# Two graph layers on one core: the order of the first and last steps, a factor row made on TensorE, and one final check

## The chip, the cores and the metric

The kernel runs on one core of a Trainium2 chip. The metric is the device time of one execution in microseconds. Before the change it is 3325.57 us, the median of three runs (3324.71 to 3328.04).

## The reference

64 graphs of 256 nodes with 512 features each go through three attention steps. All numbers are float32.

```python
# layer 0, 8 heads of 64
Q, K, V = x @ W_q + b_q, x @ W_k + b_k, x @ W_v + b_v
scores = Q K^T / 8 + a_i + c_j + b_g + log(adj + 1e-9)      # a, c = x @ w_g halves
x = softmax(scores) V + x
# layer 1, attention one (8 heads), then attention two (1 head, W2), each:
h = layer_norm(x) @ W
s, t = sum(h * a_src), sum(h * a_dst)                        # per node and head
e = leaky_relu(s_i + t_j, 0.2) + adj
x = softmax(e) h + x
```

## The kernel before

**Stages of one graph.** `graph(b)` is a Python generator. Each `yield` ends a step, and `order` lists which graph runs its next step. The steps of one graph are, in this order: "load" (x and adjacency), "turn" (transposes on VectorE, the sums S for a Winograd product on GpSimd, a copy of xT stored in DRAM); "V", "V7", "V4", then the same three for Q and for K (seven block products instead of eight; `winograd`, L294 to L344); "scores" twice (four heads each, L562, with the exponentials L569 on ScalarE); "mask" twice (the exponentials times the adjacency, L583, and their sum over the two halves, L588); "sums 0" (`weight_sums`: column sums by a matmul with ones, L371, their reciprocal L378, stored to DRAM and read back spread over the partitions as R, L381 and L386; it also fetches the stored x); "product 0" (weights times V, L404); "gather 0" (products times R plus bias and x, L413 and L418, then S and the store); "tokens 1" (transposes back, L253, for the norm's mean and variance on ScalarE, and its root on GpSimd, L276); "V1", "V1 7", "V1 4"; "rows 1" (`target_rows`, L423); eight "weights" (two instructions L658 each); "sums 1", "product 1", "gather 1", "tokens 2"; "V2", "V2 7", "V2 4", "rows 2", "weights 2" (two instructions L709) and twice "product 2" (L721, L726, L728, and four output stores L737).

**Factor rows.** The leaky exponent is written as a maximum of two products, so that a row of exp(-0.8 s) over all nodes is needed on every partition. `target_rows` makes it for eight heads and for one head alike: an exponential on ScalarE (L426), a 32x32 block transpose on VectorE (L428), four stores to DRAM (L431), and a load that spreads the row over the partitions (L441).

**Weights of layer 1.** `fold_norm` folds the norm into W1 and W2 in three steps for each: "transpose" loads two vectors spread over the partitions (L175), multiplies them with W on GpSimd in four products (L181) and reduces these on VectorE (L185). "columns" makes `left` (L192, L193), multiplies on TensorE (L197), and sends the sums through DRAM (L203 to L220). "totals" scales W (L226), forms its block differences (`combine`, L128) and transposes a small tile (L231). W1's 16 loads are traced as soon as graph 1 exists or "transpose" is reached, W2's likewise with graph 2 (L843 to L848).

**What sets the order.** TensorE runs in the order written: `start`, then a `period` of 40 steps repeated for all graphs, then `finish` (L741 to L817). The instructions of the other engines, SyncE's transfers among them, are ordered by a scheduler that takes them in the order of the program as they become ready in its own model of time; on the chip every queue then runs in the order so fixed. Tiles with one tag share a fixed number of buffers. The tag "ET" (four) holds the products of `fold_norm` and the exponentials of layers 0 and 1. The tag "X2" (four) holds the spread vectors, `left`, the token form of x for the last attention, and `bad` in `note_odd`. All matmul results share one ring of eight PSUM banks.

**Checks.** Extremes of sums and exponents are kept on the way (L348, L389, L390, L733, L734). `note_odd` (L351) compares a tile with a lower and an upper bound, three instructions for each. It is called for four tiles after the last graph's "rows 2" (L858 to L863), and for `last_top` and `last_bottom` at the end (L867). From `odd` follows a count of graphs (L869 to L876) to be done again in a slower form, whose loop runs that many times.

## Time and profile before

| what | us |
|---|---|
| median of three runs | 3325.57 |
| the profiled execution | 3324.74 |
| its span, first to last instruction | 3322.9 |
| TensorE busy, 0 to 200 | 152.08 |
| TensorE busy, 200 to 3200 | 3000.00 |
| TensorE busy, 3200 to 3322.9 | 94.66 |
| VectorE busy, whole span | 2443.8 |

PE is TensorE, PEld its weight load, DVE VectorE, ACT ScalarE, POOL GpSimd, SP SyncE, whose queue issues nearly all transfers. A line of a timeline shows the start, the time until the last of the group ends, the engine and line, the operation, what it writes from what, how many there are, and in brackets how long the engine idled before it and what ended that. A line of the list of waits shows who waited for whom: us in total, how many times, the longest.

### The profile page before, as it was taken

To read this page: it belongs to the slowest core of one execution; us is meant where nothing else is said; L and a number is where in the kernel's file an instruction comes from. 1 tells how busy PE (TensorE), PEld (TensorE's weight loads), DVE (VectorE), ACT (ScalarE), POOL (GpSimd) and SP (SyncE) were. 2 spreads that over 40 slices of the span, in tenths; PEclk is the share of its full clock that TensorE was granted. 3 is DMA by queue.
4 is the path that set the end of the run, shared out by engine and by line. 5 is a ranking of instruction groups with operands and counts; after the bars stand their busy time and mean duration, and the time that the engine had idled before them with its cause. 6 is when DMAs were issued, how large, how long until landed. Compare 5 with 4: busy or idle time off the path is not lost.

```text
span 3322.9 us, 80192 instructions
## 1 busy us (share of the span) xinstructions
PE 3246.7 (98%) x31044; PEld 2746.7 (83%) x31044; DVE 2443.8 (74%) x5273; ACT 1453.7 (44%) x4039; POOL 935.3 (28%) x1247
## 2 busy tenths in 40 slices
PE   5899999999999999999999999999999999999997
PEld 3788888888888888888888888888888888888875
DVE  4667777777777777777777777777777777777775
ACT  2344444444444444444444444444444444444442
POOL 3122322322322322322322322322322323223222
PEclk8999999999999999999999999999999999999998
DMA  5324334334333334334343343343333243343332
GB/s 132 96 76 119 105 90 119 100 95 113 103 99 113 99 102 113 93 108 111 90 114 107 91 115 101 97 114 103 92 117 105 89 119 106 89 119 104 91 97 64
DMA packets 271825, 341.26 MB, mean 103 GB/s; under 512 B 108608, under 2 KB 187728, under 8 KB 271440
## 3 DMA queue, kind: packets, MB, share of 16 engines
q1 hardware_dynamic: 270672, 335.53, 35.4%
q8 instruction: 248, 4.06, 0.5%
q14 instruction: 137, 1.12, 0.1%
q10 hardware_dynamic: 768, 0.54, 0.1%
HBM read 233.61 MB, written 102.31 MB: 101 GB/s over the span
## 4 chain that ended last, share of the span: by engine, by line
PE 94%; DVE 2%; DMA 1%; SPq 1%; issue 1%; ACT 0%; POOL 0%; ACTq 0%; DVEq 0%; POOLq 0%
PE ps_a L310 20%; PE ps_a L317 14%; PE ps_num L404 13%; PE ps_b L310 10%; PE ps_b L317 7%; PE ps_sc L562 7%; PE ps_av L721 6%; PE ps_su L371 5%; PE ps_c L310 5%; PE ps_tr L253 4%; PE ps_c L317 3%; SPq L121 1%; DMA R<-kept 1%; DMA kept<-inverse 0%; DVE ET L583 0%
## 5 line engine op out<-in xcount | busy, mean ns | idle before, releaser
L658 DVE SCALAR_TENSOR_TENSOR ET<-R,f,EA 128x256 f32<-128x256 f32 x1024 | 463.2, 518 | 138.0 <-PE ps_num L404 136.9
L404 PE MATMUL ps_num<-ET,V 128*32 128x256 f32 x8192 | 466.9, 380 | 0.0
L404 PEld LDWEIGHTS ps_num<-ET,V 128*32 128x32 f32 x8192 | 264.3, 110 | 155.1 <-issue 1.3
L583 DVE TENSOR_TENSOR ET<-ET,AT 128x1024 f32<-128x1024 f32 x256 | 304.2, 1222 | 78.8 <-ACT ET L569 78.8
L569 ACT ACTIVATE ET<-ps_sc,V 128x512 f32<-128x512 f32 x512 | 303.1, 702 | 90.2 <-PE ps_sc L562 90.0
L390 POOL TENSOR_TENSOR added<-added,inverse 128x128 f32<-128x128 f32 x128 | 69.3, 541 | 861.9 <-DVE inverse L378 745.2
L310 PE MATMUL ps_a<-w,S 128*128 128x264 f32 (+1 forms) x1024 | 273.3, 389 | 1.1 <-ACT m L607 1.1
L310 PE MATMUL ps_b<-w,S 128*128 128x264 f32 (+1 forms) x1024 | 266.5, 383 | 0.0
L721 PE MATMUL ps_av<-V,ET 128*128 128x258 f32 (+1 forms) x1024 | 247.0, 385 | 5.6 <-DVE ET L709 5.6
L286 POOL TENSOR_TENSOR S<-yT 128x256 f32<-128x256 f32 x64 | 64.0, 1000 | 666.2 <-PE ps_su L371 595.5
L562 PE MATMUL ps_sc<-QT,KT 64*128 64x256 f32 x2048 | 241.2, 385 | 0.0
L310 PEld LDWEIGHTS ps_a<-w,S 128*128 128x128 f32 x1024 | 187.1, 189 | 51.4 <-issue 19.2
L562 PEld LDWEIGHTS ps_sc<-QT,KT 64*128 64x128 f32 x2048 | 193.4, 188 | 42.5 <-issue 21.8
L310 PEld LDWEIGHTS ps_b<-w,S 128*128 128x128 f32 x1024 | 193.9, 189 | 31.0
L721 PEld LDWEIGHTS ps_av<-V,ET 128*128 128x128 f32 x1024 | 187.9, 193 | 29.1 <-DVE ET L709 4.5
L413 DVE TENSOR_TENSOR ps_num<-ps_num,R 128x512 f32<-128x512 f32 x256 | 165.6, 692 | 57.3 <-DMA R<-kept 53.5
L679 POOL TENSOR_TENSOR X<-X,bw 128x512 f32<-128x512 f32 x128 | 160.0, 1270 | 164.4 <-ACT X L268 164.4
L646 DVE TENSOR_TENSOR V<-V,factors 128x256 f32<-128x256 f32 x256 | 196.0, 824 | 0.0
L270 ACT ACTIVATE ps_tr<-ps_tr,less 128x512 f32<-128x512 f32 x256 | 165.7, 647 | 0.1
L486 ACT ACTIVATE EA<-AT 128x512 f32<-128x512 f32 x64 | 40.4, 631 | 279.5 <-DVE ET L709 265.7
L614 ACT ACTIVATE V<-ps_a,rstd 128x257 f32<-128x257 f32 (+1 forms) x128 | 61.2, 478 | 220.2 <-PE ps_a L310 220.2
L588 DVE TENSOR_TENSOR total<-ET 128x1024 f32<-128x1024 f32 x128 | 153.8, 1201 | 0.0
(166 smaller groups left out, 6987.0 us busy)
## 6 DMA issues: line engine op xcount, KB each, us to landing
R<-kept SPq DMA_DIRECT2D x128, 512.0 KB
X<-in_x_dram SPq DMA_DIRECT2D x256, 128.0 KB
kept<-xT SPq DMA_DIRECT2D x64, 512.0 KB
yT<-kept SPq DMA_DIRECT2D x64, 512.0 KB
R<-kept SPq DMA_DIRECT2D x512, 64.0 KB
kept<-yT SPq DMA_DIRECT2D x64, 512.0 KB
out_dram<-X SPq DMA_DIRECT2D x512, 64.0 KB
zT<-kept SPq DMA_DIRECT2D x63, 512.0 KB
```

The lines of the kernel that those rows point to most:

```text
L270: nc.scalar.activation(pt, pt, AF.Square, bias=less[:, of], accum_out=squares[:, of])
L310: nc.tensor.matmul(to, A[:, kk, :], B[:, kk, :], start=(first and kk == 0), stop=(kk == 1), skip_group_check=not first,)
L317: nc.tensor.matmul(to[:, m * P : (m + 1) * P], B[:, kk, m * P : (m + 1) * P], A[:, kk, :], start=(first and m == kk == 0), stop=(kk == 1), ...
L371: nc.tensor.matmul(pt[32 * g : 32 * g + 32, :P], columns[:, at - 8 * i : at - 8 * i + 32], weights[:, i % 2 * P : i % 2 * P + P], start=(i ...
L404: nc.tensor.matmul(num[32 * a : 32 * a + 32, m * N : (m + 1) * N], V[:, j, a // 2, a % 2 * P + q * DH + 32 * m :][:, :32], pair[a // 2][:, ...
L413: nc.vector.tensor_tensor(both, both, R[:, q, :].unsqueeze(1).to_broadcast([P, 2, N]), ALU.mult)
L562: nc.tensor.matmul(banks[h % 2][:, o : o + N], KT[lo : lo + DH, (q + h) // 2, j * P : (j + 1) * P], QT[lo : lo + DH, (q + h) // 2, :], sta ...
L569: nc.scalar.activation(ET[:, j, i::2, :], banks[i].rearrange("p (h n) -> p h n", n=N), AF.Exp, bias=c[:, j, :],)
L583: nc.vector.tensor_tensor(ET[:, j, :, :], ET[:, j, :, :], AT[:, j, :].unsqueeze(1).to_broadcast([P, 4, N]), ALU.mult,)
L646: nc.vector.tensor_tensor(v, v, factors8[:, at : at + H // 2, :1].to_broadcast([P, H // 2, DH]), ALU.mult)
L658: nc.vector.scalar_tensor_tensor(ET[:, j, h, :], R[q][:, h, :], f[:, j, at : at + 1], EA[:, j, :], ALU.max, ALU.mult,)
L721: nc.tensor.matmul(av[:, :width], ET[:, j, t * P : (t + 1) * P], V2[:, j, n, :width], start=(j == 0), stop=(j == NT - 1),)
```

## The change

The lists `start` and `finish` hold the same steps in another order; `period` is as before. For the last graph, "rows 2" makes the factor row without DRAM: the exponential is written to a tile of its own, VectorE copies it 128 times wide, and TensorE multiplies this copy, as the stationary operand, with the identity, which leaves the row on every partition of a PSUM bank; L709 reads it there. The two tiles for the last check become one tile `extremes`, checked by one call.

```diff
-    last_top = const.tile([P, NT], F32, name="last_top")
-    last_bottom = const.tile([P, NT], F32, name="last_bottom")
-    for t in (last_top, last_bottom):
-        nc.gpsimd.memset(t, 1.0)
+    extremes = const.tile([P, 2, NT], F32, name="extremes")
+    nc.gpsimd.memset(extremes, 1.0)
...
         def target_rows(st, heads, b):
+            if heads == 1 and b == B - 1:
+                e = small.tile([P, NT], F32, name="last_rows", tag="last_rows")
+                nc.scalar.activation(e, st[:, :, 0, 0], AF.Exp, scale=-0.8)
+                wide = data.tile([P, NT, P], F32, name="wide", tag="R1")
+                nc.vector.tensor_copy(wide, e.unsqueeze(2).to_broadcast([P, NT, P]))
+                pt = ps("row")
+                for t in range(NT):
+                    nc.tensor.matmul(
+                        pt[:, t * P : (t + 1) * P], wide[:, t, :], ident, start=True, stop=True
+                    )
+                return [pt[:, :N].rearrange("p (h n) -> p h n", h=1)]
...
-                    nc.vector.tensor_tensor(last_top, last_top, rinv, ALU.max)
-                    nc.vector.tensor_tensor(last_bottom, last_bottom, rinv, ALU.min)
+                    for i, op in enumerate((ALU.max, ALU.min)):
+                        nc.vector.tensor_tensor(extremes[:, i], extremes[:, i], rinv, op)
...
         start = [
-            (0, "load"), (0, "turn"), (0, "V"), (0, "V7"), (0, "V4"), (0, "Q"), (0, "Q7"),
-            (0, "Q4"), (0, "K"), (0, "K7"), (0, "K4"), (1, "load"), (1, "turn"),
-            ("w1", "transpose"), ("w2", "transpose"), (0, "scores"), (1, "V"), ("w1", "columns"),
-            (0, "scores"), ("w1", "totals"), (0, "mask"), (0, "mask"), ("w2", "columns"), (1, "V7"),
-            (0, "sums 0"), (0, "product 0"), (1, "V4"), (0, "gather 0"), (2, "load"), (2, "turn"),
-            (1, "Q"), (1, "Q7"), (0, "tokens 1"), (1, "Q4"), (1, "K"), (1, "K7"), (1, "K4"),
-            (0, "V1"), (0, "V1 7"), (0, "V1 4"), (1, "scores"), (0, "rows 1"), ("w2", "totals"),
-            (1, "scores"), (1, "mask"), (0, "weights"), (1, "mask"), (2, "V"), (2, "V7"),
-            (1, "sums 0"), (1, "product 0"), (1, "gather 0"), (0, "weights"), (2, "V4"), (2, "Q"),
+            (0, "load"), (0, "turn"), (0, "V"), (0, "V7"), (0, "V4"), (0, "Q"), (1, "load"),
+            (0, "Q7"), (0, "Q4"), (0, "K"), (0, "K7"), ("w1", "transpose"), (0, "K4"),
+            (0, "scores"), (0, "scores"), (1, "turn"), (0, "mask"), (0, "mask"), (1, "V"),
+            (1, "V7"), ("w1", "columns"), (1, "V4"), (0, "sums 0"), (0, "product 0"),
+            (0, "gather 0"), (1, "Q"), (1, "Q7"), ("w1", "totals"), (1, "Q4"), (0, "tokens 1"),
+            (1, "K"), (1, "K7"), (2, "load"), (1, "K4"), (0, "V1"), (0, "V1 7"), (0, "V1 4"),
+            ("w2", "transpose"), (2, "turn"), (1, "scores"), (0, "rows 1"), (1, "scores"),
+            ("w2", "columns"), (1, "mask"), (0, "weights"), (1, "mask"), (2, "V"), (2, "V7"),
+            ("w2", "totals"), (1, "sums 0"), (1, "product 0"), (1, "gather 0"), (0, "weights"),
+            (2, "V4"), (2, "Q"), (0, "weights"), (0, "weights"), (2, "Q7"), (0, "weights"),
...
         finish = [
...
-            (-2, "weights"), (-1, "mask"), (-2, "weights"), (-4, "V2"), (-4, "V2 7"), (-4, "V2 4"),
-            (-1, "sums 0"), (-1, "product 0"), (-1, "gather 0"), (-4, "rows 2"), (-2, "weights"),
-            (-2, "weights"), (-2, "weights"), (-2, "weights"), (-4, "weights 2"), (-3, "product 1"),
-            (-1, "tokens 1"), (-3, "gather 1"), (-4, "product 2"), (-3, "tokens 2"), (-1, "V1"),
+            (-2, "weights"), (-2, "weights"), (-1, "mask"), (-4, "V2"), (-4, "V2 7"), (-4, "V2 4"),
+            (-1, "sums 0"), (-4, "rows 2"), (-4, "weights 2"), (-3, "product 1"), (-2, "weights"),
+            (-2, "weights"), (-2, "weights"), (-2, "weights"), (-1, "product 0"), (-1, "gather 0"),
+            (-2, "weights"), (-3, "gather 1"), (-4, "product 2"), (-1, "tokens 1"),
+            (-3, "tokens 2"), (-1, "V1"), (-1, "V1 7"), (-4, "product 2"), (-1, "V1 4"), (-3, "V2"),
...
-            (-1, "product 1"), (-3, "product 2"), (-1, "gather 1"), (-1, "tokens 2"), (-2, "V2"),
-            (-2, "V2 7"), (-2, "V2 4"), (-2, "rows 2"), (-1, "V2"), (-2, "weights 2"), (-1, "V2 7"),
-            (-1, "V2 4"), (-1, "rows 2"), (-1, "weights 2"), (-2, "product 2"), (-2, "product 2"),
-            (-1, "product 2"), (-1, "product 2"),
+            (-1, "tokens 2"), (-2, "V2"), (-2, "V2 7"), (-2, "V2 4"), (-2, "rows 2"), (-1, "V2"),
+            (-2, "weights 2"), (-1, "V2 7"), (-2, "product 2"), (-1, "V2 4"), (-1, "rows 2"),
+            (-1, "weights 2"), (-2, "product 2"), (-1, "product 2"), (-1, "product 2"),
...
-        for v in (last_top, last_bottom):
-            note_odd(v, 1e-25, 1e25)
+        note_odd(extremes.rearrange("p i t -> p (i t)"), 1e-25, 1e25)
```

Further on, both lists differ in where single steps "load", "weights", "turn", "gather" and "mask" stand. A negative number counts from the end: -1 is the last graph, -2 the one before.

## The prediction

> **What bounds the kernel.** The page first: one engine fills the span.
>
> ```profile
> span 3322.9 us, 80192 instructions
> PE 3246.7 (98%) x31044; PEld 2746.7 (83%) x31044; DVE 2443.8 (74%) x5273; ACT 1453.7 (44%) x4039; POOL 935.3 (28%) x1247
> ```
>
> The stretches say where the missing 2% lies (columns: stretch, length, busy time of PE, PEld, DVE, ACT, POOL, granted clock, DMA share, GB/s).
>
> ```profile
> 0.00:200.00 200.00, 152.08 (x1258) 121.63 (x1259) 114.13 (x216) 61.06 (x164) 50.28 (x74) 0.91 0.37 102
> 1700.00:3200.00 1500.00, 1500.00 (x14473) 1275.30 (x14471) 1127.86 (x2427) 679.37 (x1887) 427.47 (x567) 1.00 0.36 104
> 3200.00:3322.90 122.90, 94.66 (x831) 73.03 (x829) 74.59 (x210) 36.47 (x111) 30.14 (x40) 0.91 0.24 73
> ```
>
> From 200 to 3200 TensorE never idles, so nothing can be won there. It idles 47.9 us before and 28.2 after (6.9 of these follow its last matmul). The list of waits names them for the first 205 us:
>
> ```profile
> PE ps_fold L197 <- ACT left L192: 13.1, 1, 13.1
> PE ps_su L371 <- DVE total L588: 8.6, 2, 6.3
> PE ps_a L310 <- ACT u L495: 3.9, 1, 3.9
> PE ps_fold L231 <- DMA chunks<-bw: 3.6, 1, 3.6
> PE ps_tr L253 <- DVE yT L418: 2.3, 2, 2.1
> ```
>
> The timelines say why. w1's fold waits for `left` (L192), the third user of a buffer that holds the vector w1's third product on POOL reads:
>
> ```profile
> 56.39 0.30 ACT L192 COPY left<-columns 128x128 f32<-128x128 f32 x1 [13.15 <-POOL product L181]
> 49.41 9.25 POOL L181 TENSOR_TENSOR product<-w,vector 128x1024 f32<-128x1024 f32 x4 [8.46 <-DMA vector<-in_L_gnn_a_src_dram]
> 62.16 1.22 DVE L185 TENSOR_REDUCE w<-product 128x2 f32<-128x1024 f32 x1 [2.24 <-POOL product L181]
> 63.41 4.73 ACT L569 ACTIVATE ET<-ps_sc,V 128x512 f32<-128x512 f32 x8
> 82.52 1.71 PE L371 MATMUL ps_su<-total,ones 128*32 128x128 f32 x26 [6.32 <-DVE total L588]
> ```
>
> Graph 0's exponentials (L569) start at 63.41 though their scores were done at 39: `ET` shares its tag and four buffers with the products of both folds, and the first product of w2 is reduced at 62.16 + 1.22 = 63.38. So w2's fold holds graph 0 back, to 82.5. At the other end:
>
> ```profile
> 3237.11 2.15 PE L253 MATMUL ps_tr<-ident,yT 128*128 128x128 f32 x8 [4.94 <-DVE yT L418]
> 3298.38 5.28 PE L721 MATMUL ps_av<-V,ET 128*128 128x258 f32 x16 [1.51 <-DVE ET L709]
> 3307.75 5.42 PE L721 MATMUL ps_av<-V,ET 128*128 128x258 f32 x16 [4.08 <-DVE ET L709]
> 3315.66 0.37 PE L871 MATMUL ps_tr<-ident,odd 128*1 128x128 f32 x1 [2.50 <-DVE odd L358]
> ```
>
> **The start, step by step.** Up to 37.1 the order is the same. SP is busy issuing without a break to 43.8 in both (wv, wq, wk, graph 1's X and A, then w1's 16 loads): bringing (1, "load") forward gains nothing, since SP already issues it at 27.9, as soon as it can.
>
> New: w1's transpose comes before w2's and before (1, "turn"). Its two vectors leave SP at 43.85 instead of 44.41, ahead of graph 1's 512 KB store and not followed by w2's 16 loads; I take them 2 us earlier at POOL, 47.4 for 49.41 (bounds 0 and 3: the first one now takes 5.0 from issue to use). Four products of 2.3 and reductions of 1.22 then run to 57.9. `left` now finds a free buffer, so the fold's first matmuls start when two reductions are through, the rest at 57.9; 32 matmuls, 3.5 us: done at 61.5 (before: 62.8).
>
> Graph 0's scores are now both ahead of it: 37.1 to 41.0. Their exponentials wait for the first and second product of w1 instead of w2: 47.4 + 2.3 + 1.2 = 50.9 and 53.2, eight of 0.59. PSUM is a ring of 8 banks: (1, "V") takes those of the first scores, so TensorE stands from 41.0 to about 51.5, one wait of 10 for one of 13.1. V and V7 (5.2, slow at first) run into the fold. DVE meanwhile: four reductions to 57.9, four masks and two totals of 1.2 each, two puts of 0.43, some of it between the reductions: 65.5. "sums 0" (1.0) and "product 0" (3.45) end at 70.0. Before: 88.8, of which w2's columns (3.7) come later now. **Gain 88.8 - 3.7 - 70.0 = 15.1.** If the exponentials need not wait, (1, "V") is done sooner, but the reductions still bind: 68, gain 17. If DVE runs two of w2's reductions ahead of the masks, as it does now, some 5 more: gain 10.
>
> Behind it: w2's 16 loads and two vectors, at 0.64 each 11 us of SP, go while SP waits for w1's sums (45 to 61) or just after; its products need two buffers that "product 0" frees at 70, so 75 for the last; its columns are reached at about 95: hidden by 20 us. If SP keeps them behind (2, "load"), whose adjacency waits for graph 1's turn (about 66), they leave SP from 68 to 80 and are reduced by 92: a cover of 3 us. Beyond it each us late is a us lost. w2's "totals" now stand 5.2 us of matmuls (V, V7) behind its columns; w1's row shows 7.05 from the fold's end (62.76) to the chunks (69.81): a wait of 1.9, in place of the 2.28 on "sums 0" at 125.7, since both end there. w2's scaling and differences, 8 x 0.41 + 4 x 0.67 = 6.0 of DVE, lay in DVE's idle time; now they fall where DVE is full (114 to 134): I charge 1.1, bounds 0 and 6, low since only "tokens 1" stands behind. POOL's S factors can queue behind a 2.3 us product: 0 to 2, in that charge. **Start: -14.**
>
> **The end.** Product 2 of graph -4 now comes before "tokens 1" of the last graph. It wants R(-4), issued by SP at 3231.57 behind the four R loads and landed near 3235, and fills 1.7 of the wait of 4.94. But ET(-4) (1.34 of DVE) may go ahead of yT and move it by 1.6. The chain goes on through ACT (rstd), V1, rows 1, 16 weights and T0 = 3289.95, the end of (-2, "V2 4"). Bounds -2 and +0.3: I take **-1.0**. The other moves of the finish ((-1, "load") earlier, weights and masks among each other) leave TensorE's order as it was, and lie before 3224, where it is full: nothing, unless rival (e) holds.
>
> From T0 before: R(-2) lands, product 2 at T0 + 8.4; the last R at 3307.12; last matmul at 3313.2 = T0 + 23.2. Removed for the last graph: transpose, four stores (3299.25 to 3301.57), R (3303.96 to 3307.12), that is 8.1 us and five SP issues. Added: one copy on DVE (256 wide; rows of 0.42 to 0.48, say 0.4) and two matmuls, 4 passes of 0.11 as L317's eight take 0.89: 0.45; with hops 1.1. The copy's buffer is R's, free once graph -2's L709 has run, which stands before. After: product 2 of -2 moves ahead of (-1, "V2 4"), so TensorE waits 3.2 for it, to T0 + 8.4. The Trainium skill ("TensorE: Matmul & The Clock Gate", "What's actually happening") has half rate only after an idle window of about 3.4 us; by that 3.2 could stay fast and the step take 1.74. But the row at 3298.38 took 5.28 for 16, where 3.5 is full rate, after a wait of 1.51. I take the row: step 3.5; the rule would make the sum 1.7 less. V2 4 to T0 + 12.9, then ACT, copy, two matmuls (TensorE stands 1.6 of it) T0 + 15.1, product 2 of -2 to 16.9, of -1 to 20.4: 2.8 before T0 + 23.2.
>
> But DVE has its own bill: the checks called after (-1, "rows 2"), 24 instructions, 4.7 us, whose `bad` (X2 tag, four buffers, all held by the last two graphs) waits for graph -2's first out store, near 3306; then three half products 3.7, the last check. Called before "weights 2", they can even push L709 behind them (up to 4.7). Last check: one note is 6 instructions instead of 12, -0.8 at 0.14. DVE's 9.4 from 3306.2 ends at 3315.6, as before (3315.5), if nothing of it starts sooner; TensorE's side would give -3.6. Between: **-1.5**. The 6.4 from the count to the span's end stay.
>
> **Sum**: 14 + 1.0 + 1.5 = 16.5. The profiled execution took 3324.74; 3308.2. It lies 0.8 under the median 3325.57, so **3309**.
>
> **Rivals.** (a) As above, 3304 to 3313: 0.53. (b) Free exponentials and a tail set by TensorE: 17 + 2 + 5 = 24: 3301; the products' early place in every queue speaks against it. 0.20. (c) The moved fold makes its own waits (DVE's 6.0 in full, w2's reductions ahead of masks) and the checks hold L709: 10 - 2 + 1 = 9: 3317. DVE busy 16.5 of the 20 us from 120 to 140 speaks for it. 0.18. (d) Waits only change names, within 0.2% (6.7 us, about what a measurement of this kernel tells from none): 0.05. (e) Slower: the middle has no slack (1500 of 1500), and the other engines' order there follows from the start's. If it leaves even one wait per graph, of 50.2 us each, it counts some 59 times in these 3000 us: from 0.28 us a graph the gain of 16.5 is gone, at 0.45 the result is 3335. DVE at 75% there speaks against it. 0.04.
>
> Faster is (a), (b) and (c), 0.91; within 0.2% is (d), 0.05; slower is (e), 0.04. The range leaves out (d), (e) and the edges of (b) and (c), about 0.1: 3299 to 3318.
>
> **What would show it.** L569 of graph 0 starting near 51 and "product 0" ending near 70, w2's columns near 95 without a wait; full TensorE again from about 190; no SP row for the last graph's L431 and L441; L709's last pair 2 to 3 us after V2 4. Wrong if L569 still follows a reduction of w2, if TensorE waits on L231 or L253 for over 4 us after 95, if L356 runs ahead of the last L709, or if any wait stands between 200 and 3180.

## The result, and the profile after

The changed kernel takes 3319.49 us (median of 17 runs, 3314.46 to 3322.07) where the kernel before takes 3326.13 (17 runs). The ratio is 0.9981, 95% interval 0.9974 to 0.9988: 6.6 us less, where 16.5 were forecast. The profiled execution took 3316.03 us with a span of 3314.3, so it lies 3.5 below its own median, and what is read from one trace below is held against the others.

In the changed kernel the lines have moved: L310 is L309, L371 is L370, L404 L403, L253 L252, L197 L196, L185 L184, L569 L580, L588 L599, L616 L627, L709 L720, L721 L732, L871 L882, L495 L506, L507 L518. New are L429 (the row's copy), L432 (its matmuls) and L745 (the extremes).

The stretches first (stretch, length, busy time of PE, PEld, DVE, ACT, POOL, granted clock, DMA share, GB/s):

```profile
0.00:200.00 200.00, 156.63 (x1307) 127.93 (x1307) 120.21 (x227) 64.83 (x175) 54.39 (x77) 0.94 0.38 109
1700.00:3180.00 1480.00, 1480.00 (x14293) 1258.92 (x14295) 1112.87 (x2390) 667.91 (x1852) 417.85 (x556) 1.00 0.36 104
3180.00:3314.30 134.30, 106.65 (x977) 82.15 (x969) 82.07 (x227) 42.46 (x128) 34.39 (x46) 0.92 0.24 74
```

The middle is still full, at full clock (200 to 1700 too: 1500.00 of 1500.00), so whatever changed lies in the two ends; the rival in which every graph gains a wait is out. In the first 200 us TensorE is busy for 4.55 us more than before, where 14 us of idle and slow time were to go. The list of TensorE's waits over the whole span names what it waits for now (engine, tile and line, what it waited for, us in total, times, longest; rows of the first loads left out at the dots):

```profile
PE ps_a L309 <- ACT ET L580: 10.8, 1, 10.8
PE ps_av L732 <- DVE ET L720: 8.1, 3, 4.2
PE ps_a L309 <- DVE V L518: 5.6, 2, 5.1
...
PE ps_a L309 <- ACT m L506: 4.9, 1, 4.9
PE ps_a L309 <- DVE V L627: 4.7, 4, 2.5
```

The old first place, 13.1 us for `left` of w1's fold, is gone. The first row is the forecast's wait for PSUM banks ("one wait of 10"). The second row stands at the end of the kernel. The third is a wait for VectorE's puts, its copies of finished products out of PSUM; the forecast's sum holds 4.0 us of it (the fold done at 61.5, the puts at 65.5). The fourth, and the fifth, of which 2.5 us stand in the start, were not in the forecast. TensorE's timeline shows them in place, and what the clock did behind them:

```profile
66.31 2.08 PE L309 MATMUL ps_a<-wv,xT 128*128 128x257 f32 x4 [5.07 <-DVE V L518]
68.31 1.76 PE L370 MATMUL ps_su<-total,ones 128*32 128x128 f32 x32
69.90 3.63 PE L403 MATMUL ps_num<-ET,V 128*32 128x256 f32 x64
...
98.83 1.16 PE L309 MATMUL ps_a<-w,yT 128*128 128x264 f32 x4 [2.48 <-DVE V L627]
...
103.57 1.94 PE L196 MATMUL ps_fold<-w,left 128*32 128x257 f32 x32
...
113.17 2.05 PE L309 MATMUL ps_a<-wv,S 128*128 128x257 f32 x4 [4.87 <-ACT m L506]
115.02 1.92 PE L309 MATMUL ps_b<-wv,S 128*128 128x257 f32 x4
116.73 1.44 PE L309 MATMUL ps_a<-wv,S 128*128 128x257 f32 x4
```

Product 0 of graph 0 ends at 73.5 where it ended at 88.8: 15.3 us sooner, of which w2's columns (3.66 before, 1.94 now, at 103.57) are still owed. Product 0 of graph 1 ends at 122.77 where it ended at 130.25: only 7.5 us sooner. So 13.4 us were won by 73.5, and 5.9 of them were given back in the next 49 us. V4 of graph 1, 1.0 us of TensorE, stood behind product 0 before and stands ahead of it now; with this and w1's totals (0.2) counted where they are done, 14.2 us were won and 6.7 given back.

What stands ahead of the 2.48 us wait is seen on VectorE: w2's reductions (L184), which the change moved here, between the puts of graph 0's V1 (L627):

```profile
96.75 1.22 DVE L184 TENSOR_REDUCE w<-product 128x2 f32<-128x1024 f32 x1 [0.53 <-POOL product L180]
97.89 0.48 DVE L627 SCALAR_TENSOR_TENSOR V<-ps_b,rstd,u 128x264 f32<-128x264 f32 x1
98.29 0.48 DVE L627 SCALAR_TENSOR_TENSOR V<-ps_a,rstd,m 128x264 f32<-128x264 f32 x1
```

At the end of the kernel (same columns):

```profile
3289.26 3.77 PE L732 MATMUL ps_av<-V,ET 128*128 128x258 f32 x8 [3.23 <-DVE ET L720]
...
3296.07 0.71 PE L432 MATMUL ps_row<-ident,wide 128*128 128x128 f32 x4 [1.33 <-DVE wide L429]
3296.62 1.90 PE L732 MATMUL ps_av<-V,ET 128*128 128x258 f32 x8
3299.16 3.73 PE L732 MATMUL ps_av<-V,ET 128*128 128x258 f32 x16 [0.65 <-DVE ET L720]
3306.81 0.37 PE L882 MATMUL ps_tr<-ident,odd 128*1 128x128 f32 x1 [3.91 <-DVE odd L357]
```

The row's transfers are gone and the last product waits 0.65 us in place of 4.08. But the first half of graph -2's product 2, moved ahead of the last graph's V2 4, waits 3.23 us and then runs at half speed, and the transpose of the last check stands 3.91 us for VectorE.

### The profile page after: what moved, and what is told of

It is laid out like the page before. It is cut to its first block, busy times and chain, and to the rows that moved or that the text cites. A ratio compares the mean times of both kernels' runs of the same rounds, so it can differ in the third digit from the quotient of the medians.

```text
span 3314.3 us, 80184 instructions
## 1 busy us (share of the span) xinstructions
PE 3243.3 (98%) x31048; PEld 2746.2 (83%) x31048; DVE 2440.7 (74%) x5267; ACT 1452.7 (44%) x4039; POOL 935.1 (28%) x1246
## 4 chain that ended last, share of the span: by engine, by line
PE 94%; DVE 2%; SPq 1%; DMA 1%; issue 1%; ACT 0%; POOL 0%; ACTq 0%; DVEq 0%; POOLq 0%
PE ps_a L309 20%; PE ps_a L316 13%; PE ps_num L403 13%; PE ps_b L309 10%; PE ps_b L316 7%; PE ps_av L732 7%; PE ps_sc L573 7%; PE ps_su L370 5%; PE ps_c L309 5%; PE ps_tr L252 4%; PE ps_c L316 3%; SPq L120 1%; POOL product L180 0%; DMA R<-kept 0%; SPq L442 0%
## 5 line engine op out<-in xcount | busy, mean ns | idle before, releaser
L669 DVE SCALAR_TENSOR_TENSOR ET<-R,f,EA 128x256 f32<-128x256 f32 x1024 | 461.2, 516 | 136.0 <-PE ps_num L403 134.3
L403 PE MATMUL ps_num<-ET,V 128*32 128x256 f32 x8192 | 466.5, 380 | 0.0
L403 PEld LDWEIGHTS ps_num<-ET,V 128*32 128x32 f32 x8192 | 264.0, 110 | 154.9 <-issue 1.2
L580 ACT ACTIVATE ET<-ps_sc,V 128x512 f32<-128x512 f32 x512 | 303.0, 702 | 102.4 <-PE ps_sc L573 89.5
L309 PE MATMUL ps_a<-w,S 128*128 128x264 f32 (+1 forms) x1024 | 273.4, 389 | 1.1 <-ACT m L618 1.1
L309 PE MATMUL ps_b<-w,S 128*128 128x264 f32 (+1 forms) x1024 | 266.5, 383 | 0.1
L732 PE MATMUL ps_av<-V,ET 128*128 128x258 f32 (+1 forms) x1024 | 246.9, 385 | 8.1 <-DVE ET L720 8.1
L309 PEld LDWEIGHTS ps_a<-w,S 128*128 128x128 f32 x1024 | 186.9, 189 | 51.7 <-issue 19.5
L309 PEld LDWEIGHTS ps_b<-w,S 128*128 128x128 f32 x1024 | 193.8, 189 | 31.5 <-issue 0.4
L732 PEld LDWEIGHTS ps_av<-V,ET 128*128 128x128 f32 x1024 | 187.0, 193 | 31.5 <-issue 8.8
L412 DVE TENSOR_TENSOR ps_num<-ps_num,R 128x512 f32<-128x512 f32 x256 | 165.7, 692 | 52.3 <-DMA R<-kept 49.3
L309 PE MATMUL ps_a<-wv,xT 128*128 128x257 f32 x512 | 142.3, 400 | 21.1 <-ACT ET L580 10.8
L625 ACT ACTIVATE V<-ps_a,rstd 128x257 f32<-128x257 f32 (+1 forms) x128 | 61.2, 478 | 229.0 <-PE ps_a L309 229.0
## 6 DMA issues: line engine op xcount, KB each, us to landing
X<-in_x_dram SPq DMA_DIRECT2D x256, 128.0 KB
```

Source lines behind the costliest of these rows:

```text
L309: nc.tensor.matmul(to, A[:, kk, :], B[:, kk, :], start=(first and kk == 0), stop=(kk == 1), skip_group_check=not first,)
L403: nc.tensor.matmul(num[32 * a : 32 * a + 32, m * N : (m + 1) * N], V[:, j, a // 2, a % 2 * P + q * DH + 32 * m :][:, :32], pair[a // 2][:, ...
L412: nc.vector.tensor_tensor(both, both, R[:, q, :].unsqueeze(1).to_broadcast([P, 2, N]), ALU.mult)
L580: nc.scalar.activation(ET[:, j, i::2, :], banks[i].rearrange("p (h n) -> p h n", n=N), AF.Exp, bias=c[:, j, :],)
L669: nc.vector.scalar_tensor_tensor(ET[:, j, h, :], R[q][:, h, :], f[:, j, at : at + 1], EA[:, j, :], ALU.max, ALU.mult,)
L732: nc.tensor.matmul(av[:, :width], ET[:, j, t * P : (t + 1) * P], V2[:, j, n, :width], start=(j == 0), stop=(j == NT - 1),)
```

## The experiments

The table gives the medians, the ratio to the kernel before, and two marks of each trace: when the first product 2 of graph 0 starts (everything behind it is full until the end, so a change of the start shows here and nowhere later), and the time from the first product 2 of graph -5 to the end of the span (a change of the end shows here alone). From trace to trace of the same steps either mark spreads over some 4 us.

| kernel | median us (runs) | ratio, 95% interval | start mark | end length |
|---|---|---|---|---|
| before | 3326.1 (17) | 1 | 232.8 | 129.0 |
| changed | 3319.5 (17) | 0.9981 (0.9974-0.9988) | 225.4 | 128.1 |
| e1 start only | 3315.9 (7) | 0.9973 (0.9962-0.9985) | 226.4 | 126.5 |
| e2 finish only | 3331.1 (21) | 1.0018 (1.0011-1.0024) | 235.2 | 136.5 |
| e3 copies first | 3319.2 (17) | 0.9980 (0.9973-0.9987) | 226.5 | 131.6 |
| e4 fold back | 3328.3 (21) | 1.0008 (1.0002-1.0015) | 237.3 | 129.5 |
| e5 fold late | 3325.2 (13) | 0.9998 (0.9990-1.0006) | 237.0 | 127.7 |
| e6 old finish, row | 3315.4 (8) | 0.9970 (0.9959-0.9980) | 227.6 | 124.4 |
| e7 e6 + own scratch | 3315.4 (5) | 0.9965 (0.9952-0.9979) | 229.1 | 123.3 |
| e8 no row | 3324.1 (13) | 0.9995 (0.9986-1.0003) | 228.3 | 132.6 |
| e9 one step back | 3316.9 (18) | 0.9977 (0.9970-0.9984) | 227.6 | 130.5 |
| e10 copies, totals | 3319.8 (13) | 0.9988 (0.9980-0.9996) | 225.7 | 128.0 |
| e11 + reductions | 3319.1 (21) | 0.9983 (0.9976-0.9989) | 227.7 | 127.8 |
| e12 e11 + old finish | 3315.0 (9) | 0.9974 (0.9964-0.9984) | 228.8 | 123.2 |
| e13 reductions on ScalarE | 3318.8 (18) | 0.9979 (0.9972-0.9987) | 227.0 | 131.7 |
| e14 + differences on GpSimd | 3319.4 (21) | 0.9982 (0.9976-0.9989) | 228.4 | 128.9 |
| e15 e14 + old finish | 3316.6 (9) | 0.9977 (0.9967-0.9986) | 228.0 | 125.9 |
| e16 two steps back | 3318.4 (21) | 0.9982 (0.9975-0.9988) | 225.8 | 130.6 |
| e17 reciprocal first | 3319.8 (21) | 0.9983 (0.9976-0.9989) | 228.3 | 130.5 |
| e18 e17 + old finish | 3316.1 (7) | 0.9974 (0.9963-0.9985) | 228.8 | 126.4 |

The theory at the outset: the fold of w2, moved out of the first 74 us, makes new waits in the queues of VectorE, ScalarE and SP behind it, and these take back half of the start's gain. The rivals: the loss lies in the first 74 us; or in the end.

**One part alone.**

```diff
  e1: the kernel before
-        start = [ ... ]        # its own first steps
+        start = [ ... ]        # those of the changed kernel
  e2: the kernel before
-        finish = [ ... ]
+        finish = [ ... ]       # those of the changed kernel
```

> The kernel before with the changed kernel's list of first steps alone; the last steps, the factor row and the last checks are as before. Theory 1 (the new start brings 15 us by the end of the first product of graph 0 and gives half of it back behind that, by 123 us): the whole start is worth 7.4 us here too, 3318.7 where before is 3326.1, give or take 1. Theory 2 (the start is worth more, and the new end or the new row takes some of it back): 10 us or more off, 3316 or less. Theory 3 (most of the change's measured 6.6 us are the end's): 4 us off or less, 3322 or more.

> The kernel before with the changed list of last steps alone. Theory 1: the marks of the two traces give the end some 1.2 to 1.5 us (span -8.6, of which -7.4 to -7.8 stand before the last steps start); part of it is the row's and the note's, so 0 to 1.5 us off, 3324.6 to 3326.1. Theory 2 (the new end takes back): 1 to 4 us longer. Theory 3 (the end brings most): 3 to 6 us off.

By its ratio the new start alone takes 9 us off (interval 5 to 13), more than the whole change with its 6.3, though the intervals overlap; the new end alone adds 5.7 (interval 3.7 to 8). For e1 that is nearer to theory 2 than to 1; its start mark says 6.4, and the seven traces with the start as changed have a mean of 227.2 against 234.0 for the two with the old one: 6.8. For e2 theory 2 holds, and by more than it allowed. So the end does not bring 2.5 us; as an order of steps it costs. Why is read from e2's timeline:

```profile
3302.03 3.77 PE L721 MATMUL ps_av<-V,ET 128*128 128x258 f32 x8 [3.10 <-DVE ET L709]
3307.31 2.27 PE L721 MATMUL ps_av<-V,ET 128*128 128x258 f32 x8
3316.56 6.26 PE L721 MATMUL ps_av<-V,ET 128*128 128x258 f32 x16 [6.98 <-DVE ET L709]
```

Product 2 of graph -2 comes first, waits for its weights and runs at half speed, and V2 4 of the last graph, between the first two of these lines, comes some 6 us later than it could: 13.0 us behind V2 4 of graph -2, where it was 6.9. The row of the last graph starts from V2 4, goes through four stores and a load, and the last product now waits 6.98 us for it, where it waited 4.08.

**The end taken apart.** The old order of the last steps with everything else changed; the same with the checks' scratch in two buffers of its own; and the changed kernel without the row on TensorE:

```diff
  e6: the changed kernel
-        finish = [ ... ]
+        finish = [ ... ]       # those of the kernel before
  e7: e6, in note_odd
-    name="bad", tag="X2", bufs=4)
+    name="bad", tag="bad", bufs=2)
  e8: the changed kernel, in target_rows
-            if heads == 1 and b == B - 1:
-                ...
-                return [pt[:, :N].rearrange("p (h n) -> p h n", h=1)]
```

> The changed kernel with the last steps in the order of before: the new start, the row on TensorE and the one note stay. Theory A (the new order of the last steps costs, the row pays): the wait of 4.04 us ahead of the last product in the run with the new start alone falls to about 2 (copy and row matmuls), so 1 to 2 us less than that run, 3314 to 3315, and 4.5 to 5.5 less than the changed kernel. Theory B (the row and the note cost what they save, since VectorE's checks end last anyway): as the run with the new start alone, 3315.5 to 3317. Theory C (the new order pays, once the row is there): the changed kernel's 3319.5 or more.

> The kernel of the run with the new start, the old order of the last steps and the row, where the notes' scratch tile has two buffers of its own in place of the ring that the output tiles use. In the trace of after a check stands 1.4 us behind an output transfer for that ring, and TensorE waits 3.9 us for the last check. Theory A (the checks wait for the ring, and VectorE ends the span): the large checks move into idle time of VectorE, 1.5 to 2.5 us less than without. Theory B (VectorE's time, not the ring, holds them): 0.5 us or less.

> The changed kernel without the row on TensorE: the last graph's factor row goes through VectorE's turn, four stores and a broadcast load as in the kernel before; lists and note stay as changed. If the parts add up (start -9.5, finish +5.7, change as a whole -6.6) the row and the note are worth 2.8 us here, so 3322. If the row is what pays for the new order of the last steps (in the run with that order alone the last product waits 6.98 us for this row, 1.98 in the changed kernel): up to 5 us, 3324.5. If the row is hidden: 3319.5.

e6 is 3.7 us below the changed kernel by the ratios (0.9970 and 0.9981, intervals that overlap a little), and three more pairs, which differ in the order and the scratch, go the same way by their medians: e12 is 4.1 below e11, e15 2.8 below e14, e18 3.7 below e17. That is theory A in its direction; the row's gain over e1 is not shown by the times (0.9970 against 0.9973). e8 is 4.6 above the changed kernel: the row pays where the new order makes the last product wait for it, as its second reading had it. By the medians the four corners of the end are: old order 3315.9, old order and row 3315.4, new order 3324.1, new order and row 3319.5. The row is worth about nothing with the one and 4.6 with the other; the order costs 8 without it and 4 with it.

The traces show the last part of this more evenly than the times. T0 is the end of V2 4 of graph -2; the table has the us from there to the end of the span:

| | old order | new order |
|---|---|---|
| row through DRAM | 32.9 (before), 33.2 (e1) | 38.7 (e2), 37.8 (e8) |
| row on TensorE | 30.5 (e6) | 31.9 to 33.5 (changed, e3, e4, e5, e10, e11, e13, e14, e17) |
| row and own scratch | 28.1 to 28.4 (e7, e12, e15, e18) | not run |

Without the row the new order costs 5 us here. With it, it costs 2.3 against e6, whose product behind the row ran at full clock by luck (3.63 us; 5.32 in e7): at half clock e6 would stand near 32.2, and little would be left of the order's cost behind T0. The row alone is worth 2.6 us in e6, and about 1 at half clock.

e6's timeline shows the order that the forecast did not work out, old steps with the new row:

```profile
3288.35 1.13 PE L309 MATMUL ps_a<-w,xT 128*128 128x257 f32 x4 [0.58 <-DVE V L627]
3291.88 0.68 PE L432 MATMUL ps_row<-ident,wide 128*128 128x128 f32 x4 [2.40 <-DVE wide L429]
3292.40 3.63 PE L732 MATMUL ps_av<-V,ET 128*128 128x258 f32 x16
3296.68 3.73 PE L732 MATMUL ps_av<-V,ET 128*128 128x258 f32 x16 [0.65 <-DVE ET L720]
3305.57 0.37 PE L882 MATMUL ps_tr<-ident,odd 128*1 128x128 f32 x1 [5.16 <-DVE odd L357]
```

V2 4 of graph -2 starts at 3281.43 here, and the last product ends 19.0 us later; in the changed kernel it starts at 3279.69 and the product ends 23.2 later. Graph -2's row lands while the last graph's V2 runs, so nothing needs its product early. In e7 the small checks run in idle time, the wait for the last of them falls to 1.36 us, and from the last matmul to the end it is 8.8 us in place of 12.7, as theory A has it; the medians of e6 and e7 do not differ (3315.4 both), which is theory B. In e7 a check also runs ahead of the row's copy, but the row hardly waits longer for that (2.43 us against 2.40); that product 2 behind it took 5.32 us, not 3.63, is the clock's doing (last section). From T0 the scratch saves 2.2 us in the traces, in spite of that product; that the medians do not show it stays open. The new start, the row and the old last steps (e6, with or without the scratch) are by their medians the versions below both kernels, some 10 us under the one before.

**Which step.** The two products of the finish that moved ahead, put back one after the other:

```diff
  e9: the changed kernel, last steps
-    (-1, "V2 7"), (-2, "product 2"), (-1, "V2 4"), (-1, "rows 2"), (-1, "weights 2"),
+    (-1, "V2 7"), (-1, "V2 4"), (-1, "rows 2"), (-1, "weights 2"), (-2, "product 2"),
  e16: e9, and
-    (-4, "product 2"), (-1, "tokens 1"),
+    (-1, "tokens 1"), (-4, "product 2"),
```

> The changed kernel with one step of its last steps moved back: the first product 2 of graph -2 stands behind the last graph's V2 4, rows 2 and weights 2 again, as in the order before; the row and the note stay. In the trace of after TensorE waits 3.23 us for that product's weights, runs it slowly in 3.6, and reaches V2 4 only then, so that the row comes 15.4 us behind graph -2's V2 4; in the run with the whole old order it comes 9.5 us behind it. Theory (this one step is what the new finish costs): 3 to 4.5 us less than the changed kernel's 3319.5, so 3315 to 3316.5. Rival (the other early product, of graph -4 ahead of the last graph's tokens 1, costs as much: the stretch up to the end of graph -1's first product of weights and V1 is 31.9 us in place of 30.2 to 30.9): 1.5 to 3 less, 3316.5 to 3318.

> The changed kernel with two of its last steps moved back: the first product 2 of graph -2 behind the last graph's weights 2 (as in the run before with that alone), and the first product 2 of graph -4 behind the last graph's tokens 1. If these two are all that the new order of the last steps costs: as with the whole old order, 3315.4, give or take 1, 1 to 2 us below the run with one of them back. If the second is free or pays: 3317 or more.

e9 is 2.6 us below the changed kernel by the medians, which is in the rival's range, and 1.3 by the ratios, with intervals that overlap; from T0 to the end its trace takes 32.2 us for 33.4. e16 is not below e9 (3318.4), against the rival: the early product of graph -4 is free or pays a little, and graph -2's is the one that costs, if not by much. The other 1.5 us between the medians of e9 and e6 may be none, by the intervals. In the two traces the whole difference from T0 on, 1.7 us, is one product at half clock (5.32 us against 3.63).

**The start: the queues.** ScalarE's two exponentials of graph 2's adjacency put behind the copies that TensorE waited 4.87 us for; w2's fold put back to where it was; and the whole fold put later:

```diff
  e3: the changed kernel, graph 2
-                nc.scalar.activation(EA, AT, AF.Exp)
-                nc.scalar.activation(AT, AT, AF.Identity, bias=eps)
+                ...   # both traced behind the third copy of (2, "V")
  e4: the changed kernel, first steps
+    ("w1", "transpose"), ("w2", "transpose"), (0, "K4"), ... (0, "mask"), (0, "mask"), ("w2", "columns"),
  e5: the changed kernel, first steps
+    (2, "K7"), ("w2", "transpose"), ... (3, "V7"), ("w2", "columns"), ... (3, "V4"), ("w2", "totals"),
```

> The changed kernel, but ScalarE's two exponentials of graph 2's adjacency stand behind the three copies of the value products of graph 2, not ahead of them; nothing else moves. In the trace of after TensorE waits 4.87 us for the first of these copies and then runs three groups at 2.05, 1.92 and 1.44 us where 1.03 would do. Theory 1 (this queue is where a good part of the start's gain went): the wait goes, 4.9 us, and up to 2.3 us of slow matmuls with it, so 4.5 to 7 us less than the changed kernel, 3312.5 to 3315. Rival (the work behind the wait is late by itself, since VectorE's adjacency turn and the weights stand behind the row's transfer, and the wait comes back a few steps later): less than 2 us off the changed kernel, 3317.5 or more.

> The changed kernel, but the first two steps of w2's fold are back where the kernel before has them (right behind w1's first step, and behind graph 0's masks); its third step stays. Theory 1 (moving w2's fold off the first 74 us is what gains 15 us up to the end of graph 0's first product, and what loses 7 us behind it): both go, so the end of that product comes back to 84 to 89 us, the two waits of 2.48 and 4.87 us near 100 and 110 us are gone, and the time is 3321 to 3326. Rival (the first 74 us gain by the other moves, and the fold's new place only costs): the gain stays, the loss goes, 3311 to 3315.

> The changed kernel, but w2's whole fold stands later: its first step behind the sixth product of graph 2's keys, its columns behind (3, V7), its totals behind (3, V4), where TensorE has other work throughout and w2 is still ready for graph 0's V2. With it ScalarE's copies of graph 2's values stand ahead of that graph's exponentials, and VectorE's reductions of w2 are gone from in front of graph 0's V1. Theory 1 (the queues of VectorE, ScalarE and SP behind the fold take back the start's gain between 74 and 123 us): the waits of 1.5 to 2.5 us near 98 us, of 4.87 us near 113 us and of 6.3 us for w2's chunks, which took the second one's place in the run before, all go, with some 2 us of slow matmuls: 6 to 9 us less than the changed kernel, 3310.5 to 3313.5. Rival (graph 0's weights are late by their own row transfer, and TensorE waits for those instead): less than 3 us off the changed kernel, 3316.5 or more.

e4 fits theory 1 in its direction: with the fold back, product 0 of graph 0 ends at 91.5, the start mark is 237.3, and the kernel is 2.7 us slower than before. It is no clean undoing, though: the new list has graph 1's V behind the masks, so that w2's columns come ahead of V in e4, and TensorE stood 21.9 us before them with V not begun. So it does not show what the fold alone is worth up to product 0. Behind product 0 it does undo the loss: the wait for V1's put falls from 2.48 to 0.59 us, that of 4.87 is gone. From the end of graph 0's product 0 to Q4 of graph 2, the step behind graph 1's tokens, the kernel before takes 49.3 us, the changed kernel 57.2 and e4 51.2. With V4 (1.0), w1's totals (0.2) and w2's columns (1.9) counted alike, the changed kernel loses 6.7 us there and e4 2.6, so that 4.1 us come with the first two steps of w2's fold. (In e4 all this runs 18 us later, so the other engines had more time, too.) e3 is the rival's: the wait of 4.87 us went, another of 6.29 for w2's chunks (the fold's sums, back from DRAM) ended at 116.7, and the time is the changed kernel's. e5 shows more. Product 0 of graph 1 does end sooner, at 116.6 where eight traces with w2's fold at its changed place (the changed kernel, e1, e3, e6 to e9, e16) have 122.5 to 125.4; but w2's reductions then stand in VectorE's queue ahead of graph 1's yT, and TensorE waits 8.59 us for that. The fold's price was not hidden by moving it, only paid in another place, and 5.7 us were lost.

**Two waits at once, and a third.**

```diff
  e10: e3, first steps
-    ("w2", "columns"), ... (2, "V7"), ("w2", "totals"), (1, "sums 0"), (1, "product 0"),
+    ("w2", "columns"), ... (2, "V7"), (1, "sums 0"), (1, "product 0"), ("w2", "totals"),
  e11: e10, and w2's four tensor_reduce issued behind the last put of (0, "V1 4")
  e12: e11 with the old last steps and e7's scratch
```

> The changed kernel with ScalarE's copies of graph 2's values ahead of its exponentials, as in the run before, and with w2's totals step moved behind graph 1's first product, so that TensorE does not stand before w2's chunks, which took 6.3 us of wait in that run. Theory 1 (two waits lie one behind the other, and only taking both away shows the first one's worth): 3 to 6 us less than the changed kernel, 3313.5 to 3316.5; a wait of up to 2.3 us for graph 1's masks comes back, as in the kernel before. Rival (VectorE is full from 100 to 125 us, and every wait taken away comes back as a wait for one of its results): less than 2 us off, 3317.5 or more.

> As the run with the copies and totals moved, and w2's four reductions on VectorE stand behind the last put of graph 0's V1, not ahead of it. Theory 1: the wait of 1.5 to 2.5 us near 98 us falls to 0.6, 1 to 2 us less than without this, 3312 to 3315. Rival (the reductions now stand ahead of graph 1's masks and hold its sums by the same time, 4.9 us of VectorE): no less than without, or up to 3 us more.

> The moves of the run before (copies, totals, reductions), with the last steps in the order of the kernel before and the notes' scratch in two buffers of its own. If the parts add up: the old order of the last steps with its own buffers gave 3315.4, and the start's moves take 3 to 8 us more: 3307.5 to 3312.5. If VectorE is the bound of the first 125 us: 3313.5 to 3316.

The rivals hold in all three, and e12 equals e7. In e10 none of the two waits is left, and the idle time is back two steps later, ahead of graph 1's tokens:

```profile
98.96 1.16 PE L309 MATMUL ps_a<-w,yT 128*128 128x264 f32 x4 [1.55 <-DVE V L636]
112.87 0.96 PE L370 MATMUL ps_su<-total,ones 128*32 128x128 f32 x26 [1.48 <-DVE total L608]
118.63 1.13 PE L309 MATMUL ps_a<-wv,xT 128*128 128x257 f32 x4 [1.08 <-DVE V L524]
129.16 1.75 PE L252 MATMUL ps_tr<-ident,yT 128*128 128x128 f32 x8 [3.96 <-issue]
```

The tokens start at 129.2 (129.5 in the changed kernel). VectorE's timeline of the changed kernel says what they stand behind (L184, L225 and L127 are w2's fold, L669 graph 0's weights, L377 the reciprocal of graph 1's sums, L417 its yT):

```profile
110.19 0.48 DVE L669 SCALAR_TENSOR_TENSOR ET<-R,f,EA 128x256 f32<-128x256 f32 x1 [1.20 <-DMA R<-kept]
110.59 0.76 DVE L480 STREAM_TRANSPOSE AT<-A 128x256 f32<-128x256 f32 x2
...
115.89 1.68 DVE L225 SCALAR_TENSOR_TENSOR w<-w,columns,mean 128x257 f32<-128x257 f32 x4
...
120.47 0.95 DVE L377 RECIPROCAL inverse<-ps_su 128x128 f32<-128x128 f32 x1
...
128.17 1.65 DVE L417 SCALAR_TENSOR_TENSOR yT<-ps_num,columns,yT 128x256 f32<-128x256 f32 x4
```

From 91 to 131 us VectorE is busy for 35.7 of 40, and w2's fold has 11 of them: four reductions of 1.22, eight scalings of 0.42, four differences of 0.69. The first two lines also lead to the 4.87 us: the adjacency's turn (L480) stands on VectorE behind graph 1's masks and behind a weight of graph 0 that waits 1.20 us for its row's transfer, and ScalarE's exponentials and copies stand behind the turn. The theory formed anew: VectorE's work or its order, not TensorE's visible waits, sets this stretch.

**Less work on VectorE.**

```diff
  e13: e10, fold of w2
-                    nc.vector.tensor_reduce(w[:, kk, i:4:2, HD:], ..., AX.X, ALU.add)
+                    for k in range(2):
+                        nc.scalar.activation(by_head[:, k], by_head[:, k], AF.Identity,
+                            accum_out=w[:, kk, i + 2 * k, HD:])
  e14: e13, and w2's four differences by nc.gpsimd.tensor_tensor
  e15: e14 with the old last steps and e7's scratch
```

> The run with ScalarE's copies first and w2's totals later, and w2's four reductions (1.22 us each on VectorE) made on ScalarE by accumulating copies, eight of some 0.6 us. Theory (VectorE's work between 91 and 130 us sets when graph 1's yT is done, and TensorE's waits only show where it runs ahead of it): yT, at 129.5 in the three traces so far, comes 4 to 5 us sooner, near 125, and the time falls by 3 to 5 us against the changed kernel, to 3314.5 to 3316.5. Rival (graph 1's yT waits for the transfers of its sums, or for TensorE, and not for VectorE): yT stays within 1 us of 129.5, and the time at 3318.5 to 3320.

> As the run before, and w2's four differences (0.69 us each on VectorE) made on GpSimd. Theory: another 2 to 2.7 us of VectorE's time gone, yT near 122.5, the time 5 to 8 us below the changed kernel, 3311.5 to 3314.5; a part may be lost to the products of weights that TensorE then waits for. Rival: no more than the run before, since with 4.9 us gone another engine or a transfer is the last.

> As the run before, with the old order of the last steps and the notes' scratch in two buffers of its own. If the parts add up: 3315.4 less 5 to 8, 3307.5 to 3310.5. If yT is not VectorE's: 3314 to 3316.

The rival in all three; e15, at 3316.6, lies 0.6 above its range. VectorE's busy time from 91 to 131 falls from 35.7 us to 31.1 in e13, and yT still ends at 129.7; in e14 at 131.1. In e13 the sums of graph 1 end before 115, but their reciprocal is at 119.49, behind the weights, the puts and the scalings. In e14 the differences on GpSimd made VectorE's weights beside them slow. The amount of VectorE's work is not it, as long as the order stays.

**The order on VectorE.**

```diff
  e17: e10, on VectorE
+    # ten of graph 0's weights issued behind graph 1's reciprocal,
+    # w2's scalings and differences issued behind graph 1's yT
  e18: e17 with the old last steps and e7's scratch
```

> The run with ScalarE's copies first and w2's totals later, and on VectorE graph 1's reciprocal ahead of ten of graph 0's weights and of w2's scaling, which stands behind graph 1's yT. No work is left out or moved to another engine. Theory (yT hangs on sums, reciprocal, store and load of the row, and VectorE's order holds the reciprocal 3 to 4 us too late): reciprocal at about 115.6 in place of 119.3, the row back at about 121.7, yT at 124.6 in place of 129.4, and with it the time 3.5 to 5.5 us below the changed kernel, 3314 to 3316. Rival (what VectorE gives up ahead of yT comes back behind it, in the puts of V1 or in graph 2's masks): yT earlier, the time within 1.5 us of the changed kernel, 3318 or more.

> The same, with the old order of the last steps and the notes' scratch in two buffers of its own. If the parts add up: 3315.4 less 3.5 to 5.5, 3310 to 3312. If the start gains nothing by it: 3315 to 3316.5.

The reciprocal runs at 115.67, as worked out, and the tokens start at 125.44, 4 us sooner. The time does not follow, in e17 (3319.8) or in e18 (3316.1, where nothing gained at the start was 3315 to 3316.5):

```profile
125.44 1.33 PE L255 MATMUL ps_tr<-ident,yT 128*128 128x128 f32 x8 [1.04 <-issue]
132.10 2.08 PE L319 MATMUL ps_a<-xT,wq 128*128 128x128 f32 x8 [5.33 <-DVE QT L562]
```

The scalings of w2, 5.13 us of them from 125.65 on, now stand ahead of the two puts of graph 2's Q, and TensorE waits 5.33 us for a bank: the rival. With these scalings behind the puts as well it was not run. Across these runs TensorE comes to the step behind the tokens, Q4 of graph 2, at 130.7 (changed), 131.8 (e3), 130.7 (e10), 132.1 (e11), 131.3 (e13), 132.7 (e14), 132.1 (e17), whichever of the waits had been taken away.

## Why the forecast was wrong

**The middle** was read right: 1480 of 1480 us.

**The start up to product 0: 15.1 forecast, 13.4 came.** Graph 0's exponentials start at 50.95 (51 forecast), w1's fold is done at 61.2 (61.5), the bank wait is 10.84 (10), VectorE's puts end at 66.3 (65.5). What failed is "'sums 0' (1.0) and 'product 0' (3.45) end at 70.0": V4 of graph 1 stands ahead of them and was not counted, and behind the wait of 5.07 us V4 and the sums took 2.08 and 1.76 where 1.14 and 1.08 are their full rate. 3.5 us late; 1.7 came back because w2's columns run at full rate in their new place. V4 is work moved and not lost: counted so, 14.2 came.

**The start behind it: a loss of 1.1 forecast, 5.9 came** (6.7 with V4 counted so). This is the step that failed: "its columns are reached at about 95: hidden by 20 us" with "a cover of 3 us" as the worse case, and "6.0 of DVE ... I charge 1.1, bounds 0 and 6". The worse case came: SP issued five of w2's 16 loads by 53 and then stood at the adjacency until 64.5, so that the reductions ran from 92.5 to 100.1. But the columns, at 103.57 and not at 95, never waited for them. The cover was counted against the columns alone, on TensorE, while the reductions and scalings stood in VectorE's queue ahead of other results: V1's last put (2.48 us of wait), and the reciprocal of graph 1's sums. That VectorE would come late to the adjacency's turn, and through it ScalarE to the copies of graph 2 (4.87 us and 2.3 of slow matmuls), was not in the forecast at all. What is shown is that the place of the fold's first two steps makes 4.1 of the 6.7 us (e4), that several chains through VectorE end within a few microseconds of each other there, and that a later fold costs (e5). It is not shown that any one wait is *the* cause: taken away one at a time and in pairs (e3, e10, e11, e13, e14, e17), each came back as the next one, and Q4 of graph 2 came within the same 2 us. That all of w2's fold off VectorE, with the reciprocal first, would free the 6.7 us was not tried.

**The end: a gain of 2.5 forecast, a loss of 1.6 to 3.6 came.** From e1 to the changed kernel it is 3.6 by the medians and 2.7 by the ratios, whose intervals overlap; the mean end length of the nine traces with the new order and the row (129.3) lies 1.6 above that of the two with neither (127.7). The forecast for TensorE was close: last matmul at T0 + 20.4 by its working, T0 + 22.1 in the trace. Half rate behind the 3.23 us wait, taken from the row and not from the rule of the Trainium skill ("TensorE: Matmul & The Clock Gate", "What's actually happening"), was right there: 3.77 us for eight. Its fault is what it was compared with: T0 + 23.2, old order *without* the row. The old order *with* the row ends at T0 + 17.9 (e6; T0 + 19.6 in e7, where the product behind the row ran at half clock). So the order was taken as part of the gain and was a loss of 2.5 to 4.2 us of TensorE's time under it. Of "I take **-1.0**" for graph -4's early product nothing is seen. From the end of the last graph's product 0 to its V1 the seven traces with the old order take 9.4 to 12.2 us and the twelve with the early product 10.6 to 11.9; in the changed kernel it still waited 4.18 us for its weights. Put back by itself (e16) it does not gain either: 1.5 above e9, with intervals that overlap. "**-1.5**" for the tail came as +0.5 in the profiled pair and as -0.3 in the mean of those nine traces (32.8 from T0 to the end, 33.1 in the two with neither): from the last matmul to the span's end it is 11.4 us where it was 9.7, because VectorE's checks end it, as the forecast had it for its own upper end.

**The rivals.** (c), the moved fold making its own waits, came nearest, by way of VectorE as it says; 3317 was its time, 2.5 us under the median. That it is so near is luck in part. Graph 0's masks, which it had behind w2's reductions, run at 57.71 without them, and its checks that hold L709 did not come: the first check starts at 3299.81, behind L720. Neither has it the new order as a loss. (d), "waits only change names", has the right size (6.6 us, within its 6.7) and describes e3 to e17, but not the change: the start as a whole won some 7 us. (a) and (b) are out. (e) is out.

## What to carry over

Work moved off the critical engine's list is not hidden because that engine has other work by then: count it in the queue of the engine that does it, against every result behind it, and price it there. A wait that a trace shows can be one of several chains that end together; before it is credited with its length, look for what ends second, and expect the next one there. When a change has two parts that touch the same place, work out each against the old state and both corners between: here the row paid back no more than about what the new order of steps had cost.

## What the runs showed of the hardware

**Half rate after short waits, by where they fall.** With graph -2's product behind the row (e9, e16, and all with the old last steps and the row), 16 half products follow the row's matmuls after an idle time of 2.40 to 2.58 us. They took 3.63 us in e6 and 5.32, 5.32, 5.04, 5.32, 5.89 and 5.32 in e7, e9, e12, e15, e16 and e18: the same code at the same wait, near full rate once in seven. The granted clock shows why, first in e6, then in e7 (stretch, length, TensorE busy, granted clock, DMA share, GB/s):

```profile
3287.05:3290.46 3.41, 1.85 (x8) 1.00 0.12 38
3290.46:3293.87 3.41, 1.99 (x11) 1.00 0.00 0
...
3292.01:3295.42 3.41, 0.98 (x7) 1.00 0.04 12
3295.42:3298.84 3.42, 3.42 (x10) 0.50 0.00 0
```

In all twenty traces every change of the clock (308 of them) lies on a grid of 3.41 us, which starts elsewhere in each execution. At full clock, each of the 151 stretches with TensorE busy for less than 1.40 us was followed by one at half clock, and each of the 18851 with more than 1.70 by one at full clock; in between there were both. From half clock, a stretch busy for more than 2.83 us always brought the full one back. In e7 the wait lies inside one stretch, in e6 a border cuts it in two. So what looks like chance is the place of the grid. The Trainium skill ("TensorE: Matmul & The Clock Gate", "What's actually happening") has the same free-running window of 3.4 us and calls the one before half rate idle; here it may have up to 1.4 us of work in it, so that a wait of 2.4 us is enough. The scatter of the whole time goes with the clock: of the changed kernel's 17 runs, spread over 7.6 us, those with a mean granted clock of 0.990 took 3320.9 to 3322.1, those with 0.993 and 0.994 took 3314.5 to 3317.4.

**VectorE slows beside GpSimd.** Lines of e14's VectorE (graph 0's weights) from before and during GpSimd's four differences of w2 (121.75 to 126.85):

```profile
113.27 2.85 DVE L685 SCALAR_TENSOR_TENSOR ET<-R,f,EA 128x256 f32<-128x256 f32 x7
121.53 5.99 DVE L685 SCALAR_TENSOR_TENSOR ET<-R,f,EA 128x256 f32<-128x256 f32 x6
```

0.41 us each, then 1.00. In e17 the eight scalings of w2 took 5.13 us beside GpSimd's factors of yT (3.25 in e11 with GpSimd idle). The Trainium skill ("SBUF — State Buffer", "Who interferes with whom") states that a VectorE instruction with two inputs in SBUF contends with a GpSimd instruction that reads it; these rows agree, and they say why moving 2.8 us of differences to GpSimd in e14 took nothing off VectorE: six weights became 3.5 us longer.
